# Scan stage of a two-layer image model: TensorE's order of openings and output sums, and four kinds of small work moved from VectorE to GpSimd and ScalarE

## The chip, the core and the metric

One core of one Trainium2 chip runs the whole program. The metric is the device time of one execution in microseconds (us), as a median over several executions. TensorE (PE in the profile) multiplies matrices and writes PSUM, VectorE (DVE) does elementwise work and scans, ScalarE (ACT) does activations and copies, GpSimd (POOL) does elementwise work on SBUF and issues indirect DMAs, SyncE (SP) issues the other DMAs. Each engine works through its own queue in order and waits on semaphores of the others.

## The reference, cut to what matters

Two layers, each a "conv" part and a mixture of experts. The part that matters here is the conv of layer 1, a selective scan over an image of 32 x 32 pixels, 4 images (b), 256 channels (2 tiles c of 128), 16 states (s), in four directions:

```python
def _selective_scan(x, A_log, D, W_delta, b_delta, W_B, W_C):
    delta = jax.nn.softplus(x @ W_delta + b_delta)
    Bm = x @ W_B
    Cm = x @ W_C
    A = -jnp.exp(A_log)
    dA = jnp.exp(delta[..., None] * A)
    dBx = (delta * x)[..., None] * Bm[:, :, None, :]
    ...
    _, h = jax.lax.associative_scan(combine, (dA, dBx), axis=1)
    y = jnp.einsum('blcn,bln->blc', h, Cm) + x * D
    return y
...
mamba_out = (out1 + out2 + out3 + out4) / 4
```

The four directions are forward, backward, rows flipped and columns flipped. Before it stands a norm over channels, behind it (per pixel) a norm, a router with 8 experts and the mixture of layer 1.

## The kernel before, in words

The program runs, in order: attention of layer 0; the expert tiles of layer 0 (class `Tile0`, 36 tiles of 256 tokens); the scans of layer 1 (lines 1989 to 2199); the expert tiles of layer 1; the combination. The change lies in the scans and in what runs beside them.

There are 128 scans, one for each (b, c, s), in the order of the list `order`. Each works on a tile of 128 channels x 1024 pixels. `turn(k)` (L2132) writes the instructions of one turn out by hand; nothing reorders them afterwards (`manual_schedule`). In turn k, VectorE runs the forward scan of scan k (`forth`, L2065), its backward scan (`back`, L2072) straight into the PSUM tile `sum`, the two halves of the product `yc` = sum x C of scan k-1 (L2100), a scan of 32 elements (`come_in`, L2078), and the scan down the columns (`columns`, L2089). `forth` and `back` read the decays from PSUM and `uu` from SBUF; `columns` reads both its inputs from SBUF; `yc` reads `sum` from PSUM and `cb` from SBUF.

TensorE adds into `sum` with an identity as the weight: `begin` (L2054) opens both halves with a product with noughts, `columns_added` (L2094) adds the columns of scan k-1, `third` (L2085, under the profile's line L2060) adds the third direction of scan k-1 and closes it, `back` adds twice the forward scan of k (L2060), and `output` (L2101) adds `yc` of k-1 into the PSUM tile `y`. Each of these adds is two matmuls of 128 x 512 in f32; the profile records two instructions for each of them, so four in all.

GpSimd's queue in a turn holds: the product of `third` (L2083), a difference `gap` of 32 elements (L2069), the product `uu` of scan k+1 (L2048), and an indirect DMA of routed tokens where there are any (`scatter`, L1983, one in a turn; or `fetched`, L1892, up to two in a turn). ScalarE makes the decays (L2032, L2036, L2040) and a flipped copy of `uu` (L2049).

Beside the scans run generators, called **steps** here. Each turn calls `next` on them twice: once at its start, ahead of `begin`, and once behind `come_in`. They are `Prep.steps` (the channel norm and the softplus for image b+1, L1776), `routed` (`norm` and `route` of image b-1, L1678 and L1594) and `completing` (rows of layer 0's result for images 2 and 3, L1900). Their TensorE results go to a free half of the other `sum` tile, handed out by `Spare` (L2001): free from the moment that `yc` has read it until the next `begin` opens it. A step that multiplies stands in the second call; what reads its result stands in the first call of the next turn, and the next `begin` waits for that reading. `ps_m.left` is the list of halves not handed out in this turn. Of the 128 turns about half use one.

Two PSUM tiles `sum` take turns (k even, k odd). Image 0 is prepared earlier, beside the expert tiles of layer 0, by the same `Prep.steps`.

The steps that the change touches: in `norm`, the reading of the logits `raw` (L1703) and the squares (L1707); in `Prep.steps`, `lost` (L1841, L1842: what an addition of 1 loses) for each of four parts of 128 x 512, then for each part two sums (L1861, L1862) in one turn and a product (L1865) with the skip term (L1866) in the next; in `completed`, the copy out of PSUM (L1911).

Of the kernel before, what the change touches and what calls it, by code (L numbers as in the profile page):

```python
# [11 lines left out]
F32 = mybir.dt.float32  # L12
# [4 lines left out]
AF = mybir.ActivationFunctionType  # L17
ALU = mybir.AluOpType
# [3 lines left out]
P = 128  # L22
# [40 lines left out]
def metaformer(ctx: ExitStack, tc: tile.TileContext, t: dict, out: bass.AP):  # L63
# [1614 lines left out]
    def norm(b, tok, pool, psum, tag, raw_tag, d):  # L1678

        rw = rw1
        for h in range(NHALF):
            cols = ts(h, HALF)
            mean = psum.tile([P, HALF], F32, tag=tag, name="nm_mean")
            for c in range(CT):
                nc.tensor.matmul(mean, mean_w, x[b][:, c, cols], start=(c == 0), stop=(c == CT - 1))
            yield
            for c in range(CT):
                nc.vector.tensor_tensor(d[:, c, cols], x[b][:, c, cols], mean, ALU.subtract)  # L1690
            yield
        var = pool.tile([P, NT], F32, tag="nm_var", name="nm_var")
        for r in range(NT // 2):
            tp = psum.tile([P, 2, C], F32, tag=tag, name="nm_tp")
            raw = psum.tile([P, HALF], F32, tag=raw_tag, name="raw")[:, : 2 * E].rearrange("p (n e) -> p n e", e=E)
            for i in range(2):
                n = 2 * r + i
                for c in range(CT):
                    nc.tensor.transpose(tp[:, i, ts(c, P)], d[:, c, ts(n, P)], ident)  # L1699
                for c in range(CT):  # L1700
                    nc.tensor.matmul(raw[:, i], d[:, c, ts(n, P)], rw[:, c, :], start=(c == 0), stop=(c == CT - 1))  # L1701
            yield
            nc.vector.tensor_copy(lg1[:, ts(r, 2)], raw)  # L1703
            nc.scalar.copy(tok[:, ts(r, 2), :C], tp)
            for i in range(2):
                n = 2 * r + i
                nc.scalar.activation(tp[:, i], tp[:, i], AF.Square, scale=C ** -0.5, accum_out=var[:, n : n + 1])  # L1707
            yield
        ve, sd, r0, s1, s2 = (pool.tile([P, NT], F32, tag=f"nm_{i}", name=f"nm_{i}")
                              for i in ("ve", "sd", "r0", "s1", "s2"))  # L1710

        def rsqrt(dst):

            yield
            nc.scalar.activation(sd, ve, AF.Sqrt)  # L1715
            yield
            nc.vector.reciprocal(r0, sd)
            nc.vector.tensor_tensor(sd, r0, r0, ALU.mult)
            nc.vector.tensor_tensor(sd, sd, ve, ALU.mult)
            nc.vector.tensor_scalar(sd, sd, -0.5, 1.5, ALU.mult, ALU.add)  # L1720
            nc.vector.tensor_tensor(dst, r0, sd, ALU.mult)

        nc.vector.tensor_scalar(ve, var, 1e-5, None, ALU.add)
        yield from rsqrt(s1)
        nc.vector.tensor_tensor(ve, s1, s1, ALU.mult)
        nc.vector.tensor_tensor(ve, ve, var, ALU.mult)
        nc.vector.tensor_scalar(ve, ve, 1e-5, None, ALU.add)
        nc.vector.tensor_tensor(lg1, lg1, s1.unsqueeze(2).to_broadcast([P, NT, E]), ALU.mult)
        yield from rsqrt(s2)
        nc.vector.tensor_tensor(s2, s2, s1, ALU.mult)  # L1730
        yield
        for n in range(NT):
            nc.scalar.mul(tok[:, n, :C], tok[:, n, :C], s2[:, n : n + 1])
        yield
# [33 lines left out]
    class Prep:  # L1768
# [7 lines left out]
        def steps(self, room, psum, tag):  # L1776
# [62 lines left out]
            def lost(c, cols):  # L1839
                back = self.dx[:, c, cols]  # L1840
                nc.vector.tensor_scalar(back, v[:, c, cols], 1.0, 1.0, ALU.add, ALU.subtract)  # L1841
                nc.vector.tensor_tensor(back, v[:, c, cols], back, ALU.subtract)  # L1842

            for i, (c, cols) in enumerate(parts):
                zp = psum.tile([P, HALF], F32, tag=tag, name="zp")
# [12 lines left out]
            yield  # L1858
            for c, cols in parts:
                dx = self.dx[:, c, cols]  # L1860
                nc.vector.tensor_tensor(dx, dx, v[:, c, cols], ALU.add)  # L1861
                nc.vector.tensor_tensor(self.delta[:, c, cols], self.delta[:, c, cols], dx, ALU.add)  # L1862
                yield
                yield
                nc.vector.tensor_tensor(dx, self.delta[:, c, cols], xm[:, c, cols], ALU.mult)  # L1865
                nc.vector.scalar_tensor_tensor(x[b][:, c, cols], xm[:, c, cols], dsk[:, c : c + 1],  # L1866
                                               x[b][:, c, cols], ALU.mult, ALU.add)
                yield
                yield
# [27 lines left out]

    anchor = [None]

    def completed(b, h, y, psum, tag):  # L1900

        for c in range(CT):
            op = psum.tile([P, HALF], F32, tag=tag, name="op")
            for i in range(4):
                ins = nc.tensor.transpose(op[:, ts(i, P)], y[:, i, ts(c, P)], ident)
                if i == 0 and anchor[0] is not None:
                    tc.add_manual_dep(ins.ins, anchor[0].ins.name,
                                      mybir.DependencyInfo(mybir.DependencyClass.NoSync,
                                                           mybir.DependencyReason.DATA))
            yield  # L1910
            nc.vector.tensor_copy(x[b][:, c, ts(h, HALF)], op)  # L1911
            yield

    def pause(times):
# [24 lines left out]
    with ExitStack() as st:  # L1939
        Tile0, pb, ps_n = tiles_of_0(st, "m0")  # L1940

        preps = [Prep(0)]

        def room(name, shape):

            tag = "d" if name in ("xm", "ln_sq") else name
            return pb.tile([P, *shape], F32, tag=tag, name=name, bufs=1 if name == "sp" else None)

        def whole(b):
            y = [pb.tile([P, 4, C], F32, tag=f"y{h}", name="y", bufs=1) for h in range(NHALF)]  # L1950
            yield from fetched(b, y, range(NHALF))
            yield from pause(24)
            for h in range(NHALF):
                yield from completed(b, h, y[h], ps_n, "t")

        def places():
            for b in range(B):
                yield from located(b, lambda shape: pb.tile(
                    [P, *shape], F32, tag=f"at{len(shape)}", name="at", bufs=4))

        beside = [(2, places()), (FIRST, chain(whole(0), preps[0].steps(room, ps_n, "t"), lead.steps(preps[0]))), (SECOND, whole(1))]
        for i in range(USUAL):
            one_tile = Tile0(i)
            for step in ("load", "normed", "small", "turned", "hidden", "result", "store"):
                getattr(one_tile, step)()
            anchor[0] = one_tile.last
            for first_tile, steps in beside:
                if i >= first_tile - 1:
                    for _ in range(6):
                        next(steps, None)  # L1970
        for _, steps in beside:
            for _ in steps:
                pass
# [15 lines left out]
    with ExitStack() as st:  # L1989
# [22 lines left out]
        class Scan:  # L2012
# [81 lines left out]
                    nc.tensor.matmul(cols_flipped(self.sum[:, ts(h, HALF)]), ident, grid(self.hs)[:, :, ts(h, half)],  # L2094
                                     start=False, stop=False)

            def output(self, y):
                for h in range(NHALF):
                    yc = p2.tile([P, HALF], F32, tag="yc", name="yc", bufs=4)
                    nc.vector.tensor_tensor(yc, self.sum[:, ts(h, HALF)], self.cb[:, ts(h, HALF)], ALU.mult)  # L2100
                    nc.tensor.matmul(y[:, ts(h, HALF)], ident, yc, start=(self.s == 0), stop=(self.s == NS - 1))  # L2101

            def finish(self, y):
                if self.s == NS - 1:
# [9 lines left out]
        def completing():  # L2114
            yield
            for b in range(2, B):
                for h in range(NHALF):
                    y = room("numbers", [NUMBERS])[:, : 4 * C].rearrange("p (i c) -> p i c", c=C)
                    yield from fetched(b, {h: y}, (h,))
                    yield from pause(2)  # L2120
                    yield from completed(b, h, y, ps_m, "hp")

        complete = completing()
        BEHIND = 8
# [7 lines left out]
        def turn(k):  # L2132
# [3 lines left out]
            for step in steps:  # L2136
                next(step, None)
            next(complete, None)
            if 0 <= k < len(order):
                scans[k].begin()  # L2140
            if k > 0:
                scans[k - 1].columns_added()
            if 0 <= k + 2 < len(order):
                b, c, s = order[k + 2]
                scans.append(Scan(preps[b], k + 2, c, s))
                scans[k + 2].rows()
# [28 lines left out]
            if k == NS * CT:  # L2175
                assert next(complete, "end") == "end"
            if k > 0:
                scans[k - 1].output(ys[k - 1])
            if 0 <= k < len(order):
                scans[k].come_in()  # L2180
                ps_m.open(k)
                for step in steps:
                    next(step, None)
                next(complete, None)
            if 0 <= k + 2 < len(order) and order[k + 2][2] == 0:

                b, c, _ = order[k + 2]
# [229 lines left out]
```

## Time and profile before

| what | value |
|---|---|
| median of 6 runs (lowest, highest) | 4042.91 us (4031.98, 4051.82) |
| the profiled execution | 4047.2 us |
| its span | 4045.5 us |
| granted TensorE clock, mean of the span | 0.878 |
| busy: PE, DVE, ACT, POOL | 84%, 75%, 70%, 47% of the span |
| scan stage, first `forth` to last `forth` (2191.9 to 3445.0) | 1253.1 us, 127 turns |
| the shortest turn, and the commonest | 7.86 us |

The profile's page lists busy time, a chain of waits followed back from the last instruction, and the costliest groups of instructions, one line each: source line, engine, operation, output and input, shapes, count, then busy time and mean duration, then the engine's idle time ahead of them with what ended it. The timeline lists instructions in order: start, duration, engine, line, operation, and in brackets the idle time ahead of it and what ended it. The table by windows gives busy time of each engine in a stretch and the granted clock. Durations of overlapping instructions include the overlap: a scan on VectorE lasts 2.27 us, but the next one starts 2.19 us after it.

### The profile page before, as it was taken

Reading aid. Unit: us, or ns where it says so; the run is one execution under the profiler, and the core shown is the slowest. Engines: PE = TensorE matmul, PEld = TensorE weight load, DVE = VectorE, ACT = ScalarE, POOL = GpSimd, SP = SyncE. Lnnn points to the kernel's source line nnn. Section 1 sums busy time; section 2 is a strip of 40 time slices with the busy share of each in tenths; the row PEclk is TensorE's granted clock in tenths of the full one; section 3 lists DMA queues with packets and bytes.
Section 4 is the critical chain, followed back from the end, with each engine's and each line's share of the span. In section 5 each row is a group of like instructions: output and inputs, shape, how many; then the busy total and the mean of one; then the engine's idle time right before and its main releaser. Section 6 shows DMA issues by size and latency. Waiting matters only on the chain. (4 is left out here: it accounts for less than half of the span.)

```text
span 4045.5 us, 49782 instructions
## 1 busy us (share of the span) xinstructions
PE 3394.7 (84%) x17330; PEld 1898.9 (47%) x17330; DVE 3049.1 (75%) x5440; ACT 2816.9 (70%) x3748; POOL 1888.1 (47%) x1643
## 2 busy tenths in 40 slices
PE   8368888888788878886687888888888889999996
PEld 5134444534354434433564333333333333788885
DVE  2689898988999898987666899889899899411112
ACT  2889999999999998994255667767667677422222
POOL 0145554675548564765453556445445446121111
PEclk8578788788778777788798999999999999999997
DMA  9300093000000000000573333323333334555555
GB/s 294 102 1 1 1 257 92 1 1 30 12 1 1 17 17 1 1 12 22 174 216 120 119 112 127 104 101 129 105 99 126 109 104 147 192 190 187 188 191 188
DMA packets 241815, 393.71 MB, mean 97 GB/s; under 512 B 31888, under 2 KB 182160, under 8 KB 241424
## 3 DMA queue, kind: packets, MB, share of 16 engines
q1 hardware_dynamic: 218016, 340.54, 27.0%
q0 software_dynamic: 19904, 48.48, 3.7%
q8 instruction: 139, 2.28, 0.2%
q10 hardware_dynamic: 3632, 1.40, 0.1%
q14 instruction: 124, 1.02, 0.1%
HBM read 280.41 MB, written 109.94 MB: 96 GB/s over the span
## 5 line engine op out<-in xcount | busy, mean ns | idle before, releaser
L823 POOL TENSOR_SCALAR dr<-s_n,last 128x1024 bf16<-128x1024 f32 x250 | 719.0, 2892 | 732.4 <-DVE state L851 396.8
L733 ACT ACTIVATE junk_a<-s_n,state 128x1024 int8<-128x1024 f32 x448 | 514.7, 1149 | 25.2 <-DVE state L857 9.0
L2083 POOL TENSOR_TENSOR da_c<-prod,come 128x1024 f32<-128x1024 f32 x128 | 247.0, 1929 | 466.3 <-DVE h L2089 440.5
L737 DVE TENSOR_SCALAR_CACHE_REDUCE junk_v<-s_n,state 128x1024 int8<-128x1024 f32 x320 | 408.6, 1277 | 8.8
L2265 ACT ACTIVATE hid<-hp,b 128x256 f32<-128x256 f32 x288 | 133.5, 473 | 355.9 <-PE hp L2263 355.7
L784 DVE SCALAR_TENSOR_TENSOR w<-s_n,win 128x1024 f32<-128x1024 f32 x256 | 351.0, 1371 | 5.3
L787 DVE MAX8 win<-w 128x8 f32<-128x1024 f32 x256 | 314.5, 1228 | 8.8
L891 ACT ACTIVATE ex<-sT 128x1024 f32<-128x1024 f32 x256 | 246.9, 1016 | 87.6 <-PE sT L883 87.5
L2048 POOL TENSOR_TENSOR uu<-dx,bb 128x1024 f32<-128x1024 f32 x127 | 301.0, 2370 | 1.8 <-DMA bb<-bc_d 1.7
L733 ACT ACTIVATE junk_a<-s_n,guess 128x1024 int8<-128x1024 f32 x256 | 294.3, 1149 | 7.2
L2072 DVE TENSOR_TENSOR_SCAN sum<-da,uu 128x1024 f32<-128x1024 f32 x127 | 289.1, 2276 | 11.5 <-PE sum L2054 11.5
L2065 DVE TENSOR_TENSOR_SCAN h<-da,uu 128x1024 f32<-128x1024 f32 x127 | 288.2, 2270 | 1.0 <-POOL uu L2048 1.0
L2089 DVE TENSOR_TENSOR_SCAN h<-da_c,uu 128x1024 f32<-128x1024 f32 x127 | 288.6, 2272 | 0.0
L2094 PE MATMUL sum<-h,ident 128*128 128x512 f32 x512 | 257.4, 627 | 35.5 <-DVE h L2089 35.5
L2060 PE MATMUL sum<-h,twice 128*128 128x512 f32 x512 | 251.9, 615 | 41.5 <-DVE sum L2072 41.5
L901 PE MATMUL o_ps<-ex,vT 128*32 128x256 f32 x2048 | 237.7, 449 | 53.8 <-ACT ex L891 40.5
L2032 ACT ACTIVATE da_c<-delta,a_log 128x1024 f32<-128x1024 f32 x128 | 267.4, 2089 | 5.3 <-DMA rows_y<-ys 5.2
L2274 DVE TENSOR_TENSOR ys<-yp,b2e 128x512 f32<-128x512 f32 x36 | 24.9, 691 | 321.1 <-PE yp L2271 321.1
L2263 PE MATMUL hp<-xe,w 128*128 128x256 f32 x1152 | 258.6, 381 | 6.6 <-DVE xe L2251 6.4
L2276 POOL DMA_INDIRECT results<-ys,to x72 | 69.8, 970 | 409.1 <-DVE ys L2274 196.0
L767 ACT COPY s_n<-sp 128x1024 f32<-128x1024 f32 x256 | 245.1, 1003 | 17.5 <-PE sp L759 9.8
L2271 PE MATMUL yp<-w2e,hid 128*128 128x256 f32 x1152 | 255.9, 379 | 0.0
(681 smaller groups left out, 7559.4 us busy)
## 6 DMA issues: line engine op xcount, KB each, us to landing
cb<-bc_d SPq DMA_DIRECT2D x128, 512.0 KB, 4.0
bb<-bc_d SPq DMA_DIRECT2D x127, 512.0 KB, 4.9
w<-in_w SPq DMA_DIRECT2D x36, 1024.0 KB, 5.2
w2e<-in_w SPq DMA_DIRECT2D x36, 1024.0 KB, 5.5
slots_x<-zeros SPq DMA_DIRECT2D x1, 33669.0 KB, 129.2
slots_x<-zeros SPq DMA_DIRECT2D x1, 33282.0 KB, 121.9
w<-in_w SPq DMA_DIRECT2D x72, 256.0 KB, 3.2
xs<-slots_x SPq DMA_DIRECT2D x36, 261.0 KB, 3.4
```

Source lines behind the costliest of these rows:

```text
L733: nc.scalar.activation(junk, self.row(r), AF.Sign, bias=thr, scale=-1.0, accum_out=u)
L737: nc.vector.tensor_scalar(junk, self.row(r), thr, None, ALU.is_lt, ALU.add, accum_out=u)
L784: nc.vector.scalar_tensor_tensor(w, self.row(r), self.win[:, r, 0:1], self.row(r), ALU.is_gt if r < LAST_DVE else ALU.is_ge, ALU.subtract, ...
L787: nc.vector.max(out=self.win[:, r, 1:], in_=w)
L823: ins = eng.tensor_scalar(dr, self.row(r), self.last[:, r : r + 1], None, ALU.is_lt)
L2032: nc.scalar.activation(grid(self.da_c), cols_flipped(self.prep.delta[:, self.c]), AF.Exp, scale=self.decay)
L2048: nc.gpsimd.tensor_tensor(self.uu[:, 0], self.prep.dx[:, self.c], self.bb, ALU.mult)
L2065: nc.vector.tensor_tensor_scan(rows.rearrange("p r w -> p (r w)"), self.da, self.uu[:, 0], 0.0, ALU.mult, ALU.add)
L2072: nc.vector.tensor_tensor_scan(self.sum[:, ::-1], self.da[:, ::-1], self.uu[:, 0][:, ::-1], 0.0, ALU.mult, ALU.add)
L2089: nc.vector.tensor_tensor_scan(self.hs, self.da_c, self.uu[:, 1], 0.0, ALU.mult, ALU.add)
L2094: nc.tensor.matmul(cols_flipped(self.sum[:, ts(h, HALF)]), ident, grid(self.hs)[:, :, ts(h, half)], start=False, stop=False)
L2263: nc.tensor.matmul(hp[:, f % 2], self.w1[:, c, ts(f, P)], self.xe[:, c], start=(c == 0), stop=(c == CT - 1))
```

## The change

Four edits. First, when a turn's steps have taken a half of the free `sum` tile, `begin` stands behind `columns_added` on TensorE instead of ahead of it. Second, `output` is parted: VectorE's products stay where they were, the sums into `y` stand behind the second call of the steps. Third, four of the five SBUF-only operations of `Prep.steps` go to GpSimd. Fourth, ScalarE reads the logits behind the squares, the squares go to an SBUF tile instead of back to PSUM, and ScalarE copies the completed rows in the scan stage (not beside layer 0's tiles).

```diff
@@ norm
             yield
-            nc.vector.tensor_copy(lg1[:, ts(r, 2)], raw)
             nc.scalar.copy(tok[:, ts(r, 2), :C], tp)
             for i in range(2):
                 n = 2 * r + i
-                nc.scalar.activation(tp[:, i], tp[:, i], AF.Square, scale=C ** -0.5, accum_out=var[:, n : n + 1])
+                squares = pool.tile([P, C], F32, tag="nm_sq", name="nm_sq")
+                nc.scalar.activation(squares, tp[:, i], AF.Square, scale=C ** -0.5, accum_out=var[:, n : n + 1])
+            nc.scalar.copy(lg1[:, ts(r, 2)], raw)
@@ Prep.steps
                 nc.vector.tensor_scalar(back, v[:, c, cols], 1.0, 1.0, ALU.add, ALU.subtract)
-                nc.vector.tensor_tensor(back, v[:, c, cols], back, ALU.subtract)
+                nc.gpsimd.tensor_tensor(back, v[:, c, cols], back, ALU.subtract)
...
-                nc.vector.tensor_tensor(dx, dx, v[:, c, cols], ALU.add)
-                nc.vector.tensor_tensor(self.delta[:, c, cols], self.delta[:, c, cols], dx, ALU.add)
+                nc.gpsimd.tensor_tensor(dx, dx, v[:, c, cols], ALU.add)
+                nc.gpsimd.tensor_tensor(self.delta[:, c, cols], self.delta[:, c, cols], dx, ALU.add)
                 yield
                 yield
-                nc.vector.tensor_tensor(dx, self.delta[:, c, cols], xm[:, c, cols], ALU.mult)
+                nc.gpsimd.tensor_tensor(dx, self.delta[:, c, cols], xm[:, c, cols], ALU.mult)
@@ completed
-            nc.vector.tensor_copy(x[b][:, c, ts(h, HALF)], op)
+            copy(x[b][:, c, ts(h, HALF)], op)
@@ Scan
-            def output(self, y):
+            def output(self):
+                self.yc = [p2.tile([P, HALF], F32, tag="yc", name="yc", bufs=4) for h in range(NHALF)]
                 for h in range(NHALF):
-                    yc = p2.tile([P, HALF], F32, tag="yc", name="yc", bufs=4)
-                    nc.vector.tensor_tensor(yc, self.sum[:, ts(h, HALF)], self.cb[:, ts(h, HALF)], ALU.mult)
-                    nc.tensor.matmul(y[:, ts(h, HALF)], ident, yc, start=(self.s == 0), stop=(self.s == NS - 1))
+                    nc.vector.tensor_tensor(self.yc[h], self.sum[:, ts(h, HALF)], self.cb[:, ts(h, HALF)], ALU.mult)
+
+            def output_added(self, y):
+                for h in range(NHALF):
+                    nc.tensor.matmul(y[:, ts(h, HALF)], ident, self.yc[h], start=(self.s == 0), stop=(self.s == NS - 1))
@@ turn
-            if 0 <= k < len(order):
+            shared = k > 0 and len(ps_m.left) < NHALF
+            if 0 <= k < len(order) and not shared:
                 scans[k].begin()
             if k > 0:
                 scans[k - 1].columns_added()
+            if 0 <= k < len(order) and shared:
+                scans[k].begin()
...
             if k > 0:
-                scans[k - 1].output(ys[k - 1])
+                scans[k - 1].output()
             if 0 <= k < len(order):
                 scans[k].come_in()
                 ps_m.open(k)
                 for step in steps:
                     next(step, None)
                 next(complete, None)
+            if k > 0:
+                scans[k - 1].output_added(ys[k - 1])
```

`completing` passes `nc.scalar.copy`, the steps beside layer 0's tiles pass `nc.vector.tensor_copy`.

More of the change, by code (lines that the diff above doesn't have):

```diff
@@ L1898, in metaformer, with completed @@
     anchor = [None]
-    def completed(b, h, y, psum, tag):
+    def completed(b, h, y, psum, tag, copy):
         for c in range(CT):
@@ L1953, in whole @@
             for h in range(NHALF):
-                yield from completed(b, h, y[h], ps_n, "t")
+                yield from completed(b, h, y[h], ps_n, "t", nc.vector.tensor_copy)
         def places():
@@ L2120, in completing @@
                     yield from pause(2)
-                    yield from completed(b, h, y, ps_m, "hp")
+                    yield from completed(b, h, y, ps_m, "hp", nc.scalar.copy)
         complete = completing()
```

## The prediction

> **What bounds the kernel now.** The table by windows first, to find the engine of the stage that the change touches; then VectorE's waits in that stage; then the timeline of single turns.
>
> ```profile
> 2190.00:3460.00 1270.00, 1096.84 (x2760) 464.74 (x2759) 1147.44 (x1122) 876.28 (x682) 669.40 (x464) 0.98 0.35 115
> ...
> 3350.00:3437.00 87.00, 83.78 (x201) 34.38 (x200) 87.00 (x67) 68.83 (x46) 60.30 (x44) 1.00 0.49 151
> ```
>
> Columns: PE, PEld, DVE, ACT, POOL busy, clock. In the stage VectorE is busy 1147 of 1270 us. In the second stretch no step runs and VectorE is busy 87.00 of 87.00: it is the bound, at 7.86 us a turn. 127 turns of 7.86 are 998 us; the stage takes 1253. The other 255 are VectorE's extra work and these waits:
>
> ```profile
> DVE yc L2100 <- PE sum L2060: 47.1, 37, 2.8
> DVE lg L1703 <- PE sum L1701: 13.6, 12, 1.5
> DVE nm_d L1690 <- PE sum L1687: 12.1, 6, 2.0
> DVE sum L2072 <- PE sum L2054: 11.5, 26, 1.3
> DVE ln_ve L1800 <- PE sum L1797: 5.4, 6, 2.0
> ```
>
> Some 90 us, all on TensorE, all in turns whose steps use the free `sum` half. One such turn:
>
> ```profile
> 2850.98 1.26 DVE L2100 TENSOR_TENSOR yc<-sum,cb 128x512 f32<-128x512 f32 x2
> 2852.29 2.26 DVE L2089 TENSOR_TENSOR_SCAN h<-da_c,uu 128x1024 f32<-128x1024 f32 x1
> 2856.58 0.69 DVE L1690 TENSOR_TENSOR nm_d<-x,sum 128x512 f32<-128x512 f32 x1 [2.02 <-PE sum L1687]
> ...
> 2862.31 1.99 PE L2060 MATMUL sum<-h,twice 128*128 128x512 f32 x4 [0.36 <-DVE sum L2072]
> 2864.13 1.88 PE L2101 MATMUL y<-yc,ident 128*128 128x512 f32 x4
> 2865.84 1.88 PE L1687 MATMUL sum<-x,mean_w 128*128 128x512 f32 x4
> ```
>
> A block of four records occupies TensorE for 1.71 us (2864.13 to 2865.84) and its result is there after 1.88. The step's block stands behind y's, though nobody waits for y; VectorE idles 2.02 us for it.
>
> **Order on TensorE.** Call b the end of `back`. Before: twice-block at b+0.05, y at b+1.87, mean at b+3.58, its end b+5.46, `nm_d` (1.28 for both) to b+6.75, `forth` b+6.7; the next `back` ends 11.18 after this one. After: mean at b+1.87 (`yc` has read by b+1.2), end b+3.75; `columns` ends at b+3.5, so `nm_d` runs b+3.8 to 5.05 and `forth` starts at b+5.0. TensorE goes on with y (b+3.58 to 5.3), the columns' sum (to 7.02), and only then the opening, whose result takes 0.63 more (the row of L2054 ends 0.59 after its start, 0.43 is its pitch). `back` starts at b+7.65, not at b+7.2 when `forth` is done, and ends at b+9.9. So the late opening makes a new wait of 0.4 here, and TensorE's queue is the bound in such turns: 8.2 us plus the step's own block. By the same count:
>
> - norm, 3 images: two mean turns 11.18 to 9.9 (the first of a pair 9.4, its opening is early), four turns of squares (block 1.22) 10.54 to 9.4, the first of them 9.54 to 8.4: 1.8 + 1.3 + 1.1 + 3 x 1.2 = 7.8 each, with the neighbouring turns 25 in all. The logit copies (12 x 0.17 on VectorE) lie inside these turns; on ScalarE they end 1.9 us after the transposes, ahead of the late opening, and cost nothing.
> - `bp` and `zp` turns of the preparation, 6 an image: 10.53 to 9.9 for most, 11.6 to 10.2 for one; in two cases the row L2106 (`finish`) then waits 1.6 for y, now behind a block. 2.8, 2.8, and 5.0 for image 1, whose completed rows on VectorE waited 2.22 twice for ScalarE's reading of the same tile (L1911) and now stand behind it on ScalarE: 10.6.
> - mean, variance and `rb` turns of the preparation: variance (block 1.8) gains nothing (10.03 to 10.1), the others about 1 each: 6.5. Two further turns of completed rows: 1.4.
>
> Sum 43 to 44 us off.
>
> **Sums and products on GpSimd.** The nearest row for its price is a GpSimd sum of 128x512 f32, L294: median 1.05 us, against 0.67 to 0.69 on VectorE. In the scan stage 12 each of L1842, L1861, L1862, L1865 leave VectorE. L1842 lies in `zp` turns, which TensorE bounds now: no gain. A turn with two sums is 9.18 and one with the product 9.13; without them 7.86 and 8.5 (L1866, 0.75, stays). If GpSimd hides all: 12 x (1.32 + 0.63) = 23 us off, 20 with the fetches below.
>
> What hides it? From the start t of `forth`, GpSimd's queue is third t+0.25 to 2.15, gap, `uu` to t+4.9, an indirect DMA to t+6.1 (2746.06 and 2751.15 + 0.99). The sums could run t+6.1 to 8.2, and the next third would start 0.1 late. But `columns` runs t+5.66 to 7.93, with both inputs in SBUF. What such an overlap does, the trace shows once:
>
> ```profile
> 2141.87 0.68 DVE L1865 TENSOR_TENSOR dx<-delta,xm 128x512 f32<-128x512 f32 x1
> 2142.47 0.68 DVE L1862 TENSOR_TENSOR delta<-delta,dx 128x512 f32<-128x512 f32 x1
> 2143.08 2.31 DVE L1469 TENSOR_SCALAR best<-xs,every_expert 128x2 f32<-128x2 f32 x1
> ...
> 2140.89 4.46 POOL L1932 TENSOR_TENSOR lead_uu<-dx,held 128x1024 f32<-128x1024 f32 x1 [2.73 <-issue]
> ```
>
> The GpSimd product lasts 4.46 us, not 2.36 as its twin L2048; the 2.1 more are the time in which VectorE runs two-input SBUF operations back to back, to 2143.15. Then GpSimd runs and VectorE's next instruction lasts 2.31, not 0.22 (median of L1469), ending with it. They exclude each other. I take it that `columns` excludes GpSimd likewise. (The Trainium skill, SBUF — State Buffer, section "Who interferes with whom", says that a VectorE instruction with two SBUF inputs contends with a GpSimd instruction that reads SBUF; the trace agrees for the sums, with the 4.46 us, and does not show the scan. By the page the sum below holds.)
>
> Then the two sums wait to t+7.93 and the next third starts at t'+2.2 instead of t'+0.25 (t' the next `forth`). What a late third costs is in two turns with fetches:
>
> ```profile
> 2436.17 2.51 POOL L2083 TENSOR_TENSOR da_c<-prod,come 128x1024 f32<-128x1024 f32 x1
> ...
> 2440.76 1.29 DVE L2100 TENSOR_TENSOR yc<-sum,cb 128x512 f32<-128x512 f32 x2 [1.03 <-PE sum L2060]
> ```
>
> It ended 3.40 after its `forth` (2435.28) instead of 2.14, so 1.26 late, and `yc` waited 1.03: all but 0.23. So two sums cost 1.75 in the next turn, a product 0.85: a pair is 7.86 + 0.85 + 8.5 + 1.75 = 18.96 against 18.31, 0.65 more, 12 pairs 8; the turn behind each image's last product 0.7 more; and image 1's preparation shares the queue with two fetches a turn (1.0 to 2.5 us each in L1892), some 4 more. Sum 14 us on. Ends: 20 off (no exclusion), 14 + 25 on (each of the 24 turns loses one sum more, 1.05, by VectorE waiting as well).
>
> (Rule against the edit: GPSIMD Engine Reference of the Trainium skill, section "Elementwise — side-by-side cycle accounting", puts a two-input sum at 1.96 times VectorE's time. The row here is 1.05 to 0.67, 1.57 times. By the page a sum would be an estimated 1.31, and the 14 about 20.)
>
> **Beside layer 0's tiles** 16 of these operations leave VectorE too. From 2135 to 2143.15 they fill VectorE, and the tiles' `ys` (L1494) stand at 2134.13 and 2150.46, 16 apart where 4 to 10 is usual. TensorE is busy 37 of the 50 us there. I take 4 off, half of 8 us of sums; ends 8 off, and 5 on if GpSimd (12 x 1.05 of sums and products in that spell) stalls VectorE as in the rows above. The end of the program (norm of the last image beside TensorE-bound tiles): nothing.
>
> **Sum.** -43 + 14 - 4 = -33 us on the profiled 4047.2 (span 4045.5): 4014. That execution lies 4.3 above the median of the runs, 4042.9; so **4010**. I count the change from rows at full clock; turns at a clock of 0.84 to 0.86 stay 1 to 1.7 longer as now.
>
> **Rivals.**
> 1. *No exclusion between `columns` and GpSimd*: -43 - 20 - 4 = -67, 3976. For it: no scan was seen to block; uu at 2203.64 overlapped `columns` for 0.7 and lost 0.48. Against it: the 4.46. Chance 0.2.
> 2. *GpSimd dearer than counted*: both engines wait in each add turn (upper end above): -8, 4035. The queue in such a turn is full already: 1.91 + 0.27 + 2.36 + 1.1 + 2.1 = 7.7 of 7.86. Chance 0.12.
> 3. *Slower: TensorE, now the bound of some 65 turns, gets a lower clock because it idles less.* Place: the blocks between `back` and the next `back`. A turn with squares at clock 1.00 takes 10.54; the one at 2554.65, at 0.86, took 12.24. If the stage's 0.98 fell by x, 65 turns x 9.3 us x x are added; the 33 are gone at x = 5.5%, a clock of 0.926; at 0.90 the time is about 4060. Against it: the stretch at 3350 has TensorE busy 96% at 1.00. Chance 0.1.
>
> That the order does not take effect can hardly be: the turn is written by hand, and the count of free halves is read ahead of the next handing out.
>
> **Chances.** Forecast 0.58 (4000 to 4022), rivals 0.2, 0.12, 0.1. The range 3974 to 4034 leaves out rival 3, half of rival 2 and the lower edge of rival 1. A difference of 0.2% (8 us) is about what a measurement of this kernel can tell from no change. Faster 0.82 (forecast, rival 1 and a third of rival 2), same 0.08 (the rest of rival 2), slower 0.10 (rival 3).
>
> **What would show it.** Right: waits of `lg`, `nm_d`, `ve` on TensorE gone or small; `back` waiting for L2054 in more turns, by 0.4 to 1.5; norm turns of 9.4 to 9.9; `zp` turns of 9.9; L1861 and L1862 on GpSimd behind `columns`, third about 2 us late, `yc` waiting 1.7 in those turns. Wrong: GpSimd's sums beside `columns` at 1.05 (rival 1); `columns` itself longer than 2.28 (rival 2); TensorE blocks longer than 1.88 in many turns (rival 3); a `back` that waits over 2 us in most shared turns.

## The result, and the profile after

The changed kernel takes 4032.54 us (median of 20 runs, 4018.65 to 4044.99) against 4043.51 of the kernel before (45 runs): a ratio of 0.9972, with an interval from 0.9962 to 0.9981, 11 us off. The forecast was 33 us off (4010); the time lies in the range, the gain is a third of the one forecast. The profiled execution took 4034.57, span 4032.3, granted clock 0.878 as before.

The scan stage, first `forth` to last `forth`, went from 1253.1 to 1236.5 us: 16.6 off, where -43 and +14 had been forecast. VectorE's waits in this stage, in the same view as before (total, times, longest, in us; the numbers of the lines are those of the changed kernel, in `Scan` one to four higher than before):

```profile
DVE sum L2073 <- PE sum L2055: 61.6, 48, 2.4
DVE yc L2101 <- PE sum L2061: 27.9, 20, 4.9
DVE x L2110 <- PE y L2105: 7.1, 6, 2.3
...
DVE nm_d L1690 <- PE sum L1687: 1.8, 6, 0.3
```

The waits of `lg` and of `ve` are gone or down to 0.5, that of `nm_d` fell from 12.1 to 1.8. A new one stands on top: `back` waits for the late opening, 61.6 us against 11.5. The table by windows, in the columns of the prediction:

```profile
2190.00:3443.00 1253.00, 1089.07 (x2759) 456.69 (x2759) 1137.15 (x1054) 880.65 (x702) 777.04 (x513) 0.99 0.36 116
```

VectorE ran 68 instructions fewer, yet its busy time is only 10 us shorter; GpSimd ran 49 more and is busy 108 us longer. Much of what left VectorE has come back as longer instructions. A turn with two sums (VectorE's and GpSimd's lines of the timeline) shows where:

```profile
2738.25 1.00 POOL L1984 DMA_INDIRECT slots_x<-tok,slot  x1
2738.85 1.79 DVE L2079 TENSOR_TENSOR_SCAN come<-prod,gap 128x32 f32<-128x32 f32 x1
2739.27 1.27 POOL L1862 TENSOR_TENSOR dx<-dx,sp 128x512 f32<-128x512 f32 x1
2740.56 2.26 DVE L2090 TENSOR_TENSOR_SCAN h<-da_c,uu 128x1024 f32<-128x1024 f32 x1
2740.63 3.27 POOL L1863 TENSOR_TENSOR delta<-delta,dx 128x512 f32<-128x512 f32 x1
2742.75 2.26 DVE L2066 TENSOR_TENSOR_SCAN h<-da,uu 128x1024 f32<-128x1024 f32 x1
2743.86 1.90 POOL L2084 TENSOR_TENSOR da_c<-prod,come 128x1024 f32<-128x1024 f32 x1
...
2747.84 1.29 DVE L2101 TENSOR_TENSOR yc<-sum,cb 128x512 f32<-128x512 f32 x2 [0.65 <-PE sum L2061]
```

Read it from the top. GpSimd's DMA ends at 2739.25 and its first sum follows. VectorE was free at 2738.85 for `come`, a scan of 32 elements; here it lasts 1.79 and ends 0.1 behind the sum. In the same turn of the kernel before it was:

```profile
2751.61 0.21 DVE L2078 TENSOR_TENSOR_SCAN come<-prod,gap 128x32 f32<-128x32 f32 x1
```

In the changed kernel `columns` runs only behind the held `come`, at its usual 2.26, and now the second sum is the one that stands: 3.27 us, to the end of `columns` and its own 1.1 beyond. So the two engines do exclude each other, but the first to get in was GpSimd, and VectorE lost 1.6 us that the prediction did not count. The third direction's product is 0.9 late as well, and `yc` waits 0.65.

With the order of the prediction the pair of turns (two sums, then a product) was to go from 18.31 to 18.96. In the pairs behind this first one it went to 20.43 (9.57 and 10.86): 9.57 is a turn of 7.86 and the 1.71 by which `come` is longer; 10.86 is a turn of 8.5, 1.6 more for `come`, and 0.7 because of the late third.

So it is in the 16 turns of images 2 and 3. In the eight of image 1 (turns 14 to 21) there is no scatter, `come` lasts only 0.21 to 0.70, and the loss comes by another way: GpSimd's last sum of a turn waits for `columns` there too, the fetches stand behind it in GpSimd's queue, and the next third behind the fetches. In turn 21 the third starts 3.6 behind `forth` instead of 0.2, and VectorE waits for it:

```profile
2423.27 1.29 DVE L2101 TENSOR_TENSOR yc<-sum,cb 128x512 f32<-128x512 f32 x2 [4.95 <-PE sum L2061]
```

Some 1.9 of the 4.95 is TensorE's clock: in that turn the granted clock is 0.75, and the third's block takes 3.78 instead of 1.88. Turns 14 and 17 wait 3.66 and 4.30 in the same way (granted clock 0.89 and 0.87).

The late opening, in a turn with squares (VectorE and TensorE):

```profile
2879.25 1.96 PE L2105 MATMUL y<-yc,ident 128*128 128x512 f32 x4
...
2881.05 1.88 PE L2095 MATMUL sum<-h,ident 128*128 128x512 f32 x4
2882.76 0.60 PE L2055 MATMUL sum<-nought 128*128 128x512 bf16 x2
...
2883.47 2.30 DVE L2073 TENSOR_TENSOR_SCAN sum<-da,uu 128x1024 f32<-128x1024 f32 x1 [1.63 <-PE sum L2055]
```

`forth` ended near 2881.84, and `back` could have followed. The opening stands behind y's and the columns' blocks, so `back` starts at 2883.47. The turn is 9.60, against 10.54 before.

Beside layer 0's tiles (VectorE and GpSimd):

```profile
2133.84 12.74 DVE L1472 TENSOR_TENSOR wt<-best,xs 128x2 f32<-128x2 f32 x1
2134.48 2.49 POOL L1866 TENSOR_TENSOR dx<-delta,xm 128x512 f32<-128x512 f32 x2
2136.92 2.47 POOL L1862 TENSOR_TENSOR dx<-dx,sp 128x512 f32<-128x512 f32 x2
2139.35 2.47 POOL L1863 TENSOR_TENSOR delta<-delta,dx 128x512 f32<-128x512 f32 x2
2141.79 2.47 POOL L1866 TENSOR_TENSOR dx<-delta,xm 128x512 f32<-128x512 f32 x2
```

An operation on two numbers a row (0.15 for its neighbours) lasts 12.74 us, as long as GpSimd has operations standing one behind the other (the last of them, L1933, ends at 2146.56). Two `ys` (L1494) of the tiles are 29.3 us apart there, against 16.3 at most before.

### The profile page after: what moved, and what is told of

Read it like the earlier page. It is cut to its first block, busy times and chain, and to the rows that moved or that the text cites. A ratio compares the mean times of both kernels' runs of the same rounds, so it can differ in the third digit from the quotient of the medians.

```text
span 4032.3 us, 49811 instructions
## 1 busy us (share of the span) xinstructions
PE 3387.7 (84%) x17330; PEld 1890.4 (47%) x17330; DVE 3047.5 (76%) x5352; ACT 2820.7 (70%) x3772; POOL 2013.3 (50%) x1707
## 5 line engine op out<-in xcount | busy, mean ns | idle before, releaser
L2073 DVE TENSOR_TENSOR_SCAN sum<-da,uu 128x1024 f32<-128x1024 f32 x127 | 289.6, 2280 | 61.7 <-PE sum L2055 61.6
L2095 PE MATMUL sum<-h,ident 128*128 128x512 f32 x512 | 246.3, 604 | 56.5 <-DVE h L2090 55.8
L2061 PE MATMUL sum<-da_c,ident 128*128 128x512 f32 x512 | 250.7, 613 | 31.0 <-POOL da_c L2084 29.4
L2041 ACT ACTIVATE da<-delta,a_log 128x1024 f32<-128x1024 f32 x128 | 142.9, 1116 | 170.6 <-DVE sum L2073 170.6
```

The costliest lines, as they stand in the source:

```text
L2061: nc.tensor.matmul(self.sum[:, ts(h, HALF)], ident if eye is None else eye, view[:, ts(h, HW // NHALF), :], start=False, stop=last)
L2073: nc.vector.tensor_tensor_scan(self.sum[:, ::-1], self.da[:, ::-1], self.uu[:, 0][:, ::-1], 0.0, ALU.mult, ALU.add)
```

## The experiments

Theory A: the order on TensorE brings what was forecast, and the loss is GpSimd's: its sums reach SBUF first and VectorE stands. Rivals: the order brings less than counted, or TensorE's clock falls. The first four kernels stand beside 4046.19 us of the kernel before, the next four beside 4048.35, the last two beside 4046.78; ratios are to those.

**order_only**: the changed kernel with the four operations of the preparation back on VectorE.

```diff
-nc.gpsimd.tensor_tensor(back, v[:, c, cols], back, ALU.subtract)
+nc.vector.tensor_tensor(back, v[:, c, cols], back, ALU.subtract)
... (the two sums and the product likewise)
```

> Theory (the order on TensorE brought what was forecast, and GpSimd's operations gave it back): about 43 us faster than before, some 4000; the scan stage from first to last forward scan 1209 to 1211 us, the turns with two sums back at 9.2 and those with the product at 9.1, no small scan of 0.2 us longer than 0.25. Rival (the order itself brought only what the changed kernel shows, and GpSimd's part costs nothing): 11 us faster, like the changed kernel.

4003.86 us, ratio 0.9897 [0.9867, 0.9926]: 42 off, scan stage 1213.9, so 39.2 off (42 to 44 expected). The order brings about what was forecast. The turns with two sums are back at 9.19, those with the product at 9.13, and no `come` lasts over 0.23.

**gpsimd_only**: the kernel before with the same four operations on GpSimd.

> Kernel before with the four operations of the preparation on GpSimd and nothing else. Theory: slower than before by about 35 us, 27 in the scan stage and 8 beside layer 0's tiles; the small scan L2078 stands 1.6 to 1.8 us for GpSimd's first sum in the turns with sums. Rival (GpSimd's part costs nothing, the order brought little): within 8 us of before.

4084.09, ratio 1.0098 [1.0078, 1.0119]: 38 us slower, 31.5 of them in the scan stage (35 and 27 expected). This edit by itself is a loss larger than the change's whole gain.

**y_late_only**: the kernel before with only `output` parted, y's sums behind the steps.

```diff
-                scans[k - 1].output(ys[k - 1])
+                scans[k - 1].output()
...
                 next(complete, None)
+            if k > 0:
+                scans[k - 1].output_added(ys[k - 1])
```

> Kernel before with y's sums behind the steps on TensorE, openings where they were, nothing else. Theory (the late opening takes back part of what y's place brings): 55 to 58 us faster than before, so more than the order as a whole. Rival (both halves of the order add up): less than the 43 of the whole order, 20 to 25.

3986.61, ratio 0.9857 [0.9835, 0.9879]: 60 off, scan stage 1195.2. This part alone brings more than the four parts together.

**opening_late_only**: the kernel before with only `begin` behind `columns_added` in shared turns.

> Kernel before with the openings behind the columns' sum in shared turns, nothing else. Theory: some 20 us faster than before, because TensorE adds the columns while it would wait for the readers of the free half. Rival: slower, because the backward scan waits for the later opening and y's sums still stand ahead.

4033.58, ratio 0.9978 [0.9963, 0.9992]: some 9 to 13 off where some 20 were expected; scan stage 1239.1, 14 off.

Each order edit gains alone, and together (with ScalarE's reading, in order_only) they gain less than the first alone. The next two take the late opening away again.

**order_early_opening**: order_only with `begin` ahead of the columns' sum in every turn.

```diff
-            shared = k > 0 and len(ps_m.left) < NHALF
+            shared = False
```

> Order and ScalarE's part of the change, all operations of the preparation on VectorE, but every opening ahead of the columns' sum as before. Theory (beside y's late sums the late opening only makes the backward scan wait): some 62 to 67 us faster than before, 20 to 24 faster than with the late openings. Rival (the openings' place does not matter once y is late): like the run with the order alone, 42 faster.

3980.76, ratio 0.9838 [0.9825, 0.9851]: 68 off, scan stage 1180.9. A turn with squares, as above, now 8.58 (VectorE and TensorE):

```profile
2847.14 1.96 PE L2105 MATMUL y<-yc,ident 128*128 128x512 f32 x4
2847.94 2.27 DVE L2066 TENSOR_TENSOR_SCAN h<-da,uu 128x1024 f32<-128x1024 f32 x1
2848.94 0.38 PE L2055 MATMUL sum<-nought 128*128 128x512 bf16 x1
2849.37 1.88 PE L2095 MATMUL sum<-h,ident 128*128 128x512 f32 x4
2850.12 2.27 DVE L2073 TENSOR_TENSOR_SCAN sum<-da,uu 128x1024 f32<-128x1024 f32 x1
```

`back` follows `forth` without a wait. Once y's sums stand behind the steps, the step's block is done early, its readers too, and the early opening holds `back` up by no more than 0.7 us in any turn; the late one puts two blocks ahead of `back`.

This kernel differs from y_late_only by ScalarE's part of the change alone. That part is worth 14 us by the stage of the two traces (1195.2 against 1180.9); by the runs it is not told from nothing, as the intervals of 0.9857 and 0.9838 overlap.

**order_early_y_last_first**: the same, but behind the last state (s = 15) of a tile, where `finish` reads y in the next turn, y's sums go ahead of the steps again.

```diff
                 scans[k - 1].output()
+            if k > 0 and scans[k - 1].s == NS - 1:
+                scans[k - 1].output_added(ys[k - 1])
...
-            if k > 0:
+            if k > 0 and scans[k - 1].s < NS - 1:
                 scans[k - 1].output_added(ys[k - 1])
```

> As the run with the early openings, and y's sums of the last of 16 states ahead of the steps, since VectorE's finish waits for them (2.34 twice in the changed kernel). Theory: 2 to 5 us faster than that run. Rival: no difference that can be measured.

3972.2, ratio 0.9811 [0.9799, 0.9824]: 76 off, the fastest version here. By the stage it is 2.7 better than order_early_opening (1178.2); the intervals of the two nearly touch. `finish` waits 2.4 us in all, against 6.1 there.

**image0_on_vector**: the changed kernel with the preparation of image 0, the one beside layer 0's tiles, on VectorE.

```diff
-nc.gpsimd.tensor_tensor(
+(nc.gpsimd if b else nc.vector).tensor_tensor(
```

> The changed kernel with the preparation of image 0, beside layer 0's tiles, on VectorE as before; images 1 to 3 on GpSimd. Theory (GpSimd's ten operations one behind the other there keep VectorE's two-input instructions out): 8 us faster than the changed kernel, 19 faster than before; no instruction of 12 us on VectorE. Rival (the spell is hidden beside the tiles): like the changed kernel, 11 faster than before.

4028.05, ratio 0.9954 [0.9936, 0.9972], scan stage 1236.3 as in the changed kernel. No VectorE instruction there lasts over 2.31. First to last `ys` is 219.7 us in the changed kernel, 223.0 in gpsimd_only and 218.6 in come_behind_columns (below), but 211.7 to 216.8 in the kernel before and the eight versions with this work on VectorE: by the means, 220.4 and 214.6, about 6 us lost. The ratios, 0.9954 and 0.9972, are 7 us apart too, but their intervals overlap, so it is the trace that carries this.

**spare_gpsimd_work**: order_only, and in single turns without steps one spare GpSimd instruction on a tile of its own.

```diff
+            if kind == "sum":
+                nc.gpsimd.tensor_tensor(scratch[:, :size], scratch[:, :size], scratch[:, :size], ALU.mult)
+            else:
+                nc.gpsimd.memset(scratch.bitcast(BF16)[:, :size], 1.0)
```

> The order alone, and in single turns without steps one further GpSimd instruction on a tile of its own, ahead of the small scan. A turn without it lasts 7.86. Theory (a GpSimd instruction that reads SBUF and VectorE's small scan, which reads two SBUF tiles, exclude each other, and a sum queued behind an indirect DMA holds VectorE from before its own start): product of 512 columns behind the DMA (turns 114, 116, 126) 9.5; the same ahead of the DMA (122) and without a DMA (28) 8.3 to 8.5; product of 64 columns behind the DMA (124) 8.5 to 8.7; a memset of the same length (118, 120), which reads nothing, 7.86. Rival A (any GpSimd work stalls VectorE): the memset turns are 9.5 too. Rival B (the exclusion lasts only as long as the recorded instruction): 114 and 124 are 7.9 to 8.2, since the small scan is over when the recorded product begins, and the columns' scan is the one that waits or goes first.

One run, 4019.59; the turns are what is read. Without spare work 7.86. A product of 512 columns behind the scatter: 9.36, 9.33 and 9.33, `come` 1.71, 1.68 and 1.67. A memset, which reads nothing, 1.39 us long: 7.86, `come` 0.21. The product ahead of the scatter 8.10, in a turn without a scatter 8.10, `come` 0.45 in both (8.3 to 8.5 expected); it starts 0.7 ahead of `come` there and ends 0.4 behind `come`'s start. So one instruction that reads SBUF costs 1.5 us of a turn where it stands behind the scatter, and one that only writes nothing. But 64 columns behind the scatter cost 0.04, where 8.5 to 8.7 was expected: there `come` and `columns` went first and the product lasted 1.97.

**spare_gpsimd_sizes**: the same frame, with other sizes.

> All sums and products on VectorE; in single turns without steps one spare GpSimd instruction stands behind the scatter: products of 64 columns (turns 114 and 124), 128 (116), 256 (118), 384 (120), a copy of 512 columns with one input (122) and a product of 512 from two different tiles (126). Theory A (by size: a longer instruction has the ports already while the scatter ahead of it is in work): `come` lasts 0.2 and the GpSimd instruction about 2 us for the small sizes, and from some size on `come` lasts 0.5 + the GpSimd instruction's own time, up to 1.8 for 512, the copy too. Rival B (whoever is ready first by a few hundredths of a us, whatever the size): no order by size; the same 64 columns come out differently in turns 114 and 124, or all sizes like 512. Rival C: it takes two inputs; then the copy leaves `come` at 0.2.

One run, 4006.59. Pairs of lines (VectorE's `come`, GpSimd's spare instruction) of the timeline, by size:

```profile
3303.93 0.25 DVE L2079 TENSOR_TENSOR_SCAN come<-prod,gap 128x32 f32<-128x32 f32 x1
...
3304.47 1.97 POOL L2188 TENSOR_TENSOR scratch<-scratch 128x64 f32<-128x64 f32 x1
...
3335.56 0.56 DVE L2079 TENSOR_TENSOR_SCAN come<-prod,gap 128x32 f32<-128x32 f32 x1
...
3336.08 2.62 POOL L2188 TENSOR_TENSOR scratch<-scratch 128x256 f32<-128x256 f32 x1
...
3351.71 1.46 DVE L2079 TENSOR_TENSOR_SCAN come<-prod,gap 128x32 f32<-128x32 f32 x1
3352.25 0.84 POOL L2188 TENSOR_TENSOR scratch<-scratch 128x384 f32<-128x384 f32 x1
...
3400.76 1.92 DVE L2079 TENSOR_TENSOR_SCAN come<-prod,gap 128x32 f32<-128x32 f32 x1
3401.30 1.29 POOL L2190 TENSOR_TENSOR scratch<-inner,scratch 128x512 f32<-128x512 f32 x1
```

It goes by size, and 64 columns come out alike both times (`come` 0.25 and 0.24). Up to 256 columns `come` is held by 0.04 to 0.35 us and the GpSimd instruction ends 0.1 to 0.4 behind `columns`; at 384 and 512 `come` is held by 1.25 to 1.7 and GpSimd's instruction runs through. A copy of 512 columns, one input, acts like a product of 256 (0.55 and 2.61), so what counts looks like the amount read; two readings at that amount are few. In each of them `come` is longer from a time ahead of the recorded start of GpSimd's instruction, while the scatter ahead of it is still in work. Why the short ones let VectorE in is not settled.

**come_behind_columns**: the changed kernel with `come` behind `columns` on VectorE. It tells whether the small scan is the trouble, or whatever VectorE has in that place.

```diff
-                scans[k].come_in()
                 ps_m.open(k)
...
                 scans[k].columns()
+                scans[k].come_in()
```

> The changed kernel with the small scan `come` moved behind `columns` on VectorE, so that `columns` itself stands where `come` stood, ready while GpSimd works on the scatter ahead of its first sum. Theory A (whatever VectorE has ready there is held, because GpSimd's sum takes the ports first): `columns` lasts 3.5 to 3.9 us instead of 2.27 in the turns of image 2 and 3 with sums or products, a pair of such turns stays at 20.2 to 20.6, and the time stays at that of the changed kernel, a ratio of 0.996 to 0.998 to the kernel before. Rival B (the order of the prediction was right and only the small scan upset it): `columns` goes first at 2.27, both sums wait behind it, a pair falls to about 19.0, the 12 pairs give back some 13 us, ratio 0.993 to 0.995. Under both, turns without such work grow by at most 0.1, since `third` may start 0.2 late without cost.

4041.74, ratio 0.9989 [0.9976, 1.0002], where 0.996 to 0.998 was expected. A turn with two sums, VectorE's and GpSimd's lines:

```profile
2736.38 3.98 DVE L2090 TENSOR_TENSOR_SCAN h<-da_c,uu 128x1024 f32<-128x1024 f32 x1
2736.93 1.27 POOL L1862 TENSOR_TENSOR dx<-dx,sp 128x512 f32<-128x512 f32 x1
2738.28 3.15 POOL L1863 TENSOR_TENSOR delta<-delta,dx 128x512 f32<-128x512 f32 x1
2740.28 1.23 DVE L2079 TENSOR_TENSOR_SCAN come<-prod,gap 128x32 f32<-128x32 f32 x1
```

Now `columns` is held: 3.98 us instead of 2.27, and `come` is held by the second sum. A turn with the product holds L1867, the skip term, instead (2.38, not 0.75) and `columns` goes free. A pair takes 20.77 (10.60 and 10.17), a little above the 20.2 to 20.6 expected. Rival B, `columns` first and a pair of 19.0, has fallen: in that place the first sum goes ahead of whatever VectorE has there with two SBUF inputs.

## Why the prediction was right and wrong

**Order on TensorE and ScalarE's reading, -43.** Right in mechanism, and in size partly by luck: order_only measures 42 off, and in the changed kernel the turns without sums and products lost 43.6. By turns, forecast and measured: mean turns 9.9 and 9.4, measured 9.96 and 9.46; squares 9.4 and 8.4 for the first, measured 9.60 and 8.38; `zp` 9.9, measured 9.96. But some 5 of the 43.6 are TensorE's clock, which the sum left as it was: three norm turns of the trace before (36, 70 and 103) had a granted clock of 0.85 to 0.86 and took 1.7 more than their like (12.24 against 10.54 in two of them), and none of the changed kernel's did. On the other side the mean, variance and `rb` turns brought 4.1, not 6.5. `back`'s wait was forecast at 0.4 to 1.5: 0.38 in mean turns, 1.63 with squares, up to 2.37 in four turns with `bp`. `finish` waits 2.3 in two turns, forecast 1.6. Nor did all of the 90 us of waits lie in turns whose steps use the free half: 4.1 of `yc`'s lay in turns 15, 23, 24 and 112, which use none. What the sum did not ask is whether the late opening is needed beside late sums: order_early_opening against order_only shows that it costs some 25 us there (33 by the stage of the traces).

**Sums and products on GpSimd, +14.** This is the step that failed: "I take it that `columns` excludes GpSimd likewise. ... Then the two sums wait to t+7.93". The exclusion is real, and the second sum does wait for `columns`; but for the first sum, and for the product, the order is the other way. `come` has two SBUF inputs as well, which the step overlooked, and it stands ahead of `columns`; but come_behind_columns shows that the small scan is not the whole of it: behind the scatter GpSimd's first sum goes ahead of `columns` too. VectorE is held 1.6 to 1.7 us in each of the 16 turns of images 2 and 3 with a sum or product, a cost that the step put at nothing (its upper end allowed 1.05), and the late third, on which it put the whole cost, is a smaller one: 0.9 late behind two sums, not 2, and on time behind a product.

Measured by turns, the turns with these operations grew by 27.0 us; the others fell by 43.6, and the stage by the 16.6 of the trace. Of the 27.0, 18.3 lie in images 2 and 3, where the prediction's own terms give 6.6 (eight pairs at 0.65, and 0.7 twice). Image 1 grew by 8.8, where they give 7.3 (four pairs, 0.7 and the 4 for the fetches): that part was near, though the lower clock in three of its turns, which the terms do not hold, has a share in the 8.8. After against order_only gives 22.6 for the same edit: its other turns are 4.5 shorter, 2.2 of this in three `zp` turns that carry L1842 on VectorE without it (11.02 against 10.30). The kernel before loses 31.5, 29.2 of them in the same turns.

(The Trainium skill, SBUF — State Buffer, section "Who interferes with whom", says that issue order, not the shape of the operation, decides who blocks, and calls the shared ports an exclusive lock. Of the 512-column sums the traces agree with the lock: `come` at 1.79 ends 0.1 behind the sum, and `columns` at 3.98 runs its 2.2 from the sum's end. Which of the two was issued first they can't show, as `come` is recorded as starting 0.4 ahead of the sum that holds it. Of the shape they differ: in the same place of both queues, products up to 256 columns let VectorE in after 0.04 to 0.35 us and end last.)

The price of a sum was off as well: 1.05 was taken from a sum of other operands, and the rows here are 1.27 to 1.29. The page on GpSimd that the prediction weighed, the GPSIMD Engine Reference of the Trainium skill, section "Elementwise — side-by-side cycle accounting", had given an estimated 1.31, nearer than the row.

**Beside layer 0's tiles, -4.** Wrong in sign: about 6 lost, near the 5 of its own upper end. The rows of 4.46 and 2.31 us in the prediction's own fence had shown that operations on one engine can shut the other out to their end; moved to GpSimd, the queue shuts VectorE out, 12.74 us once.

**The sum.** -43.6 and +27.0 in the scans and +6 beside the tiles make about -11; measured -11. Of the rivals, the first (no exclusion) is refuted by every add turn of images 2 and 3. The second came nearest, in time (4035) and in mechanism: both engines wait in those turns, though `columns` is not what grew, as it had it. The third is refuted for the stage as a whole: the clock there is 0.99 against 0.98. It fell anew where TensorE had idled for a late third (turns 14, 17 and 21), not where it idled less.

## What to carry to other kernels

Where two engines exclude each other, ask which of them is in first, and list everything that the other has ready in that stretch with two SBUF inputs, however small: an instruction moved off the bound engine can hold that engine for longer than it ran there. Order a shared engine's queue by who waits for each result, one edit at a time: y's sums put last brought 60 us, and the late opening, a gain by itself, cost some 25 beside it. The fastest version has both lessons in it: all of the preparation on VectorE, an early opening, y's sums last but where `finish` reads them, 0.9811 of the kernel before.

## What the runs showed of the hardware that was not expected

- A VectorE scan with both inputs in SBUF and a GpSimd instruction that reads SBUF exclude each other: beside a GpSimd sum or product of 512 columns behind a scatter, 32 elements took 1.67 to 1.93 us instead of 0.21, and 128x1024 took 3.98 instead of 2.27. In turn, a sum that came second took 3.27 instead of 1.27. A GpSimd memset beside them cost nothing (`come` 0.21).
- A GpSimd product behind an indirect DMA held VectorE from about 0.5 us ahead of its recorded start (3400.76 against 3401.30), at 384 columns and more to its end, at 256 and fewer for 0.35 and less. Ahead of the DMA, or without one, 512 columns cost `come` 0.24.
- A queue of GpSimd operations without a gap kept a two-element VectorE operation out for 12.74 us: it was not let in between two of them.
